# Layer 0 of a conv-attention hybrid: the second norm as a factor per token behind its linear layer, the projection's bias added by VectorE, and a new fixed order

## The chip, the cores and the metric

The kernel runs on one core of a Trainium2 chip. The metric is the device time of one execution in microseconds; the median of the runs is given. All tensors are float32.

## The reference, cut to what matters

The input x is 2 x 128 x 64 x 64 (images, channels, rows, columns). Layer 0 is a neighbourhood attention with a small feed-forward part, layer 1 is a full self-attention over the 4096 tokens of an image and a long filter. The change touches layer 0 alone:

```python
def _ln(x, g, b):
    mu = jnp.mean(x, -1, keepdims=True)
    var = jnp.mean((x - mu) ** 2, -1, keepdims=True)
    return (x - mu) * jax.lax.rsqrt(var + 1e-05) * g + b

r = x
y = _ln(x, g1, be1)
y = _na2d(y, qkv_w, qkv_b, rpb, proj_w, proj_b)   # 7x7 window, 4 heads; ends with out @ proj_w.T + proj_b
y = _ln(y, g2, be2)
y = y @ w1.T + bl1
x = y + r
r = x
y = _ln(x, g3, be3)
y = y @ w2.T + bl2
y = jax.nn.relu(y)
y = _ln(y, g4, be4)
y = y @ w3.T + bl3
x = y + r
```

The input of this is a group norm of x, and its result is added to x. Each norm is over the 128 channels of one token.

## The kernel before, in words

**Bands.** Layer 0 works on 16 bands: 2 images times 8 groups of 8 rows, 512 tokens each. Channels lie on the partitions (128 x 512); a norm over channels therefore transposes the band into four tiles of 128 tokens x 128 channels, takes mean and variance per token, and transposes back. Gains of the norms are multiplied into the weights once at the start, and the norms' constant terms become biases (`weights`, line 702 on).

**Pieces.** The work of a band is cut into named pieces. `p.*` makes the first norm and q, k, v (v goes to DRAM, `vd`, and comes back as windows, `vw`, through SP's queue). `u0` to `u3` are four units of 128 queries: `S` scores, `t0`-`t3` bias tables and row minimum on VectorE (line 517), `e0`-`e3` exp on ScalarE (line 527), `T0`, `T1` transposes (line 540), `c0`, `c1` their copies to SBUF (line 547), `V` the product with v (line 562). `r.*` scales by the denominators: `r.rb` on GpSimd (line 579), `r.rdT`, `r.c`, `r.att` (line 593). `t.*` is the rest:

- `t.proj` (lines 598 and 600): a 128 x 512 matmul of a one-hot row with `prow` puts the projection's bias into PSUM, four 128-column matmuls add onto it.
- norm `t1` (statistics `bn`, GpSimd's power `pw`, `nb`, `z` of two token tiles on ScalarE `za`, of two on VectorE `zd`, four transposes `tr`, copy `zT`), linear `t.w1`, residual `t.x2` (line 614).
- `t.tx` transposes x2 to tokens, norm `t2`, linear `t.w2` (line 331), `t.y` Relu with bias on ScalarE (line 635), `t.ty` transposes y to tokens (line 326), norm `t3`, `t.w3`, `t.fin` adds onto x.
- `t.add` on GpSimd (lines 624 and 626) adds the last bias and the outer residual to x2 in place.

`k.*` (bands 8 to 15 only) prepares layer 1's tokens of image 0: `k.a`, `k.tt`, `k.bn`, `k.pw`, `k.z` (GpSimd, line 683), `k.b` (transposes), `k.cm`.

**Order.** TensorE, VectorE, ScalarE and GpSimd each run a fixed order. The table `PLAN` gives each piece a time within a band's course; band k's pieces are shifted by k times `PERIOD`, all pieces are sorted by that time, and each engine executes its instructions in this order. So pieces of up to six bands are mixed. The first two bands' `p` pieces, the weights (`w`), the flips of the position table (`f0`-`f3`) and the table subtractions (`tab`) follow the list `FIRST`. Pieces of the last bands beyond a certain point (63 of them) are left to the attention of layer 1, whose loop calls three of them at each step; there the order is the compiler framework's. PSUM has five banks for most pieces, two more for some transposes and the projection, and one for `V`.

**Start.** SP issues eight DMAs for x of image 0 (line 126), then weights, the table rows (line 276), the masks and later x of image 1; ScalarE's queue issues the table rows of head 0 (line 278). The group norm's statistics come from x as it lands.

Of the kernel before, what the change touches and what calls it, by code (L numbers as in the profile page):

```python
# [14 lines left out]
P = 128  # L15
NB = 2
T = 4096
# [31 lines left out]

PLAN = {  # L50
    "p.xg": -4624, "p.tok": -4623, "p.bn": -4585, "p.pw": -4482, "p.zd": -4151, "p.nb": -3839, "p.za": -3660,
    "p.tr": -3511, "p.zT": -3413, "p.q": -3201, "p.k": -2932, "p.kT": -2885, "p.qT": -2796, "p.v": -2549,
    "p.vc": -2382, "u0.S": 0, "u0.t1": 36, "u0.t3": 47, "u0.t0": 54, "u0.t2": 62, "u0.e1": 108, "u0.e3": 138,
    "u0.e2": 138, "u0.e0": 219, "u0.T1": 464, "k.a": 508, "u0.T0": 531, "k.tt": 547, "u0.c0": 647, "u0.c1": 737,
    "u1.S": 780, "u1.t2": 906, "u1.t0": 946, "u1.t1": 951, "u1.t3": 1087, "u1.e1": 1088, "k.bn": 1103,
    "u2.S": 1108, "u2.t3": 1115, "u1.e3": 1128, "u2.t1": 1198, "u2.t0": 1198, "u2.e3": 1200, "u2.t2": 1274,
    "u2.e1": 1310, "u2.e0": 1339, "u1.e2": 1405, "u2.e2": 1786, "u2.T0": 1850, "u2.T1": 1865, "u1.e0": 1890,
    "u2.c1": 1906, "u1.T0": 1940, "u1.T1": 1979, "u0.V": 1986, "u2.c0": 1990, "u1.c0": 2005, "u1.c1": 2060,
    "u3.S": 2115, "u1.V": 2198, "u3.t3": 2222, "u3.t2": 2233, "u3.t1": 2278, "u3.t0": 2278, "k.pw": 2308,
    "u3.e1": 2339, "u3.e0": 2364, "u3.e3": 2372, "u3.e2": 2384, "u2.V": 2397, "r.rden": 2420, "u3.T0": 2436,  # L60
    "r.rb": 2566, "u3.c0": 2608, "u3.T1": 2689, "u3.c1": 2783, "r.rdT": 2827, "r.c": 2898, "u3.V": 2937,
    "k.z": 3009, "r.att": 3184, "t.proj": 3500, "k.b": 3601, "t1.bn": 3713, "k.cm": 4033, "t1.pw": 4306,
    "t1.nb": 4348, "t1.zd": 4410, "t1.za": 4597, "t1.tr": 5531, "t1.zT": 5674, "t.w1": 6276, "t.x2": 6324,
    "t.tx": 6935, "t2.bn": 7341, "t2.pw": 7594, "t2.nb": 7773, "t.add": 7929, "t2.za": 7975, "t2.zd": 7996,
    "t2.tr": 8384, "t2.zT": 8719, "t.w2": 9610, "t.y": 9723, "t.ty": 10247, "t3.bn": 10697, "t3.pw": 10918,
    "t3.zd": 11092, "t3.nb": 11166, "t3.za": 11410, "t3.tr": 11496, "t3.zT": 11553, "t.w3": 11573,
    "t.fin": 11589,
# [5 lines left out]
    "gn p.xg0 p.xg1 p.tok0 f0 p.tok1 p.bn0 f1 p.bn1 p.pw0 w f2 p.zd0 p.nb0 p.za0 p.pw1 p.tr0 f3 p.zd1 p.nb1 p.za1 p.zT0"  # L73
    " tab p.tr1 p.v0 p.q0 p.k0 p.vc0 p.zT1 p.qT0 tab0 p.kT0 tab1 p.v1 p.k1 p.q1 p.vc1 p.kT1 p.qT1 tab2 tab3"
# [18 lines left out]
def kernel(  # L93
# [31 lines left out]
    for c in range(8):  # L125
        nc.sync.dma_start(out=xa[0][:, c * 512 : (c + 1) * 512], in_=xin[0, :, c * 512 : (c + 1) * 512])
# [12 lines left out]

    nc.gpsimd.memset(rev[:, 0].rearrange("p n m -> p (n m)"), 0.0)  # L140
    nc.vector.memset(rev[:, HEADS - 1, NTAB], 0.0)
# [3 lines left out]
    flip = const.tile([P, P], F32, name="flip")  # L145
    nc.gpsimd.memset(flip, 0.0)
    nc.gpsimd.affine_select(
        out=flip, in_=flip, compare_op=ALU.not_equal, fill=1.0, base=1 - P, pattern=[[1, P]], channel_multiplier=1,
# [72 lines left out]
    with l0a:  # L221
# [26 lines left out]
        def flipped(h):  # L248
            pb = l0_bank()
            for half in range(2):  # L250
                nc.tensor.matmul(
                    pb[half * 64 : (half + 1) * 64, 0 : NTAB * NTAB], lhsT=flip[0:64, 64:128],
                    rhs=rev[:, h, 0:NTAB].rearrange("p n m -> p (n m)"), start=True, stop=True,
                )
            nc.scalar.copy(base[:, h].rearrange("p n m -> p (n m)"), pb[:, 0 : NTAB * NTAB])
# [14 lines left out]
        for r in range(QT):  # L270
            lo = 6 - min(r, 6)
            src = bass.AP(
                rpb_pad.tensor, (RPR + r - 6) * RPW + 50, [[1, QT], [RPW, (HEADS - 1) * RPR - r // 7], [1, NTAB]]
            )
            rows_ = rev[r * QT : (r + 1) * QT].rearrange("p h n m -> p (h n) m")
            nc.sync.dma_start(out=rows_[:, RPR : HEADS * RPR - r // 7], in_=src)
            src = bass.AP(rpb_pad.tensor, (lo + r - 6) * RPW + 50, [[1, QT], [RPW, RPR - lo], [1, NTAB]])
            nc.scalar.dma_start(out=rows_[:, lo:RPR], in_=src)
        nc.sync.dma_start(out=mask, in_=nc.inline_tensor(_window_masks(), "window_masks").ap())
# [13 lines left out]
        e0 = wp.tile([P, P], F32, name="e0")  # L293
        nc.gpsimd.memset(e0, 0.0)
        nc.gpsimd.memset(e0[0:1, :], 1.0)
        prow = wp.tile([P, 4, P], F32, name="prow")
        nc.gpsimd.memset(prow.rearrange("p j c -> p (j c)"), 0.0)
        wg = w_sb
        cb = wp.tile([P, 6], F32, name="cb")
        C_Q, C_K, C_V, C_1, C_2, C_3 = range(6)  # L300
# [68 lines left out]
        def norm_pieces(stage, src):  # L369
# [11 lines left out]
            @piece(stage + "pw")  # L381
            def _(t, b, g):
                rs = t[stage + "rs"] = ls.tile([P, 4], F32, tag="ln_rs", name="ln_rs")
                nc.gpsimd.tensor_scalar(rs, t[stage + "mv"][:, :, 1], 1e-5, None, ALU.add)
                nc.gpsimd.tensor_tensor(rs, rs, mhalf[:, 0:4], ALU.pow)

# [38 lines left out]
        @piece("p.xg")  # L425
        def _(t, b, g):
            gm, grs = norms[b]
            eng = nc.vector if b == 0 and g < 2 else nc.gpsimd
            t["xg"] = bp.tile([P, BAND], F32, tag="xg", name="xg", bufs=5)
            for nat, til in ordered(xa[b][:, rows_of(g)], t["xg"]):  # L430
                eng.tensor_scalar(til, nat, gm, grs, ALU.subtract, ALU.mult)
# [62 lines left out]
        def unit_pieces(u):  # L494
# [40 lines left out]
            def half_pieces(ch):  # L535
# [9 lines left out]
                def _(t, b, g):  # L545
                    pT = t[f"{name}c{ch}"] = sp.tile([HK, 512], F32, tag=f"pT{ch}", name="pT")
                    (nc.vector.tensor_copy if ch else nc.scalar.copy)(pT, t[f"{name}T{ch}"][0:HK])
# [48 lines left out]
        def _(t, b, g):  # L596
            pt = t["pp"] = l0_bank(1)
            nc.tensor.matmul(pt, lhsT=e0, rhs=prow.rearrange("p j c -> p (j c)"), start=True, stop=False)
            for j in range(4):
                nc.tensor.matmul(  # L600
                    pt[:, j * P : (j + 1) * P], lhsT=t["att"][:, j * P : (j + 1) * P],
                    rhs=wg[:, W_PROJ : W_PROJ + P], start=False, stop=(j == 3),
                )

        norm_pieces("t1.", "pp")
# [14 lines left out]
        norm_pieces("t2.", "px")  # L620
# [8 lines left out]
        def _(t, b, g):  # L629
            t["p2"] = linear(W_2, t["t2.zT"])  # L630

        @piece("t.y")
        def _(t, b, g):
            t["y"] = bp.tile([P, BAND], F32, tag="y", name="y", bufs=1)
            nc.scalar.activation(t["y"], t["p2"], AF.Relu, bias=cb[:, C_2 : C_2 + 1])  # L635

        @piece("t.ty")
        def _(t, b, g):
            t["py"] = to_tokens(t["y"])

        norm_pieces("t3.", "py")
# [55 lines left out]
        def weights():  # L697

            for i, (lo, be, col, row) in enumerate((
                (W_QKV, V_BE1, V_QB, None), (W_QKV + P, V_BE1, V_KB, None), (W_QKV + 2 * P, V_BE1, None, R_VB),
                (W_1, V_BE2, None, R_BL1), (W_2, V_BE3, None, R_BL2), (W_3, V_BE4, V_BL3, None),
            )):
                pb = l0_bank()
                nc.tensor.matmul(
                    pb[:, 0:1], lhsT=w_sb[:, lo : lo + P], rhs=v_sb[:, be : be + 1], start=True, stop=row is None
                )
                if row is None:  # L710
                    nc.vector.tensor_tensor(cb[:, i : i + 1], pb[:, 0:1], v_sb[:, col : col + 1], ALU.add)
                else:
                    nc.tensor.matmul(pb[:, 0:1], lhsT=r_sb[:, row, :], rhs=ones[:, 0:1], start=False, stop=True)
                    nc.vector.tensor_copy(cb[:, i : i + 1], pb[:, 0:1])
            pb = l0_bank()
            nc.tensor.matmul(
                pb[0:1, 0:P], lhsT=cb[:, C_V : C_V + 1], rhs=w_sb[:, W_PROJ : W_PROJ + P], start=True, stop=True
            )
            for j in range(4):
                nc.vector.tensor_tensor(prow[0:1, j, :], pb[0:1, 0:P], r_sb[:, R_PROJ, :], ALU.add)  # L720
            for lo, hi, g in ((W_QKV, W_PROJ, V_G1), (W_1, W_2, V_G2), (W_2, W_3, V_G3), (W_3, 896, V_G4)):
                nc.vector.tensor_scalar(wg[:, lo:hi], w_sb[:, lo:hi], v_sb[:, g : g + 1], None, ALU.mult)

            nc.vector.tensor_scalar(cb[:, 0:1], cb[:, 0:1], -QSCALE, None, ALU.mult)

# [9 lines left out]
        for name, f in (  # L735
            ("gn", lambda: [None for _ in group_norm(0)]), ("w", weights),
# [5 lines left out]
        for i in range(8):  # L742
            events.append((2 * PERIOD + 600 * i, None, "", lambda ci=2 + i // 4, h=i % 4: table(ci, h, nc.gpsimd)))

# [8 lines left out]
        free = ("r.att", "t.x2", "t.y", "t.fin")  # L753
        held = (("r.att", "t.proj", 1), ("t.x2", "t.fin", 4), ("t.y", "t.ty", 1))
# [644 lines left out]
```

## Time and profile before

| what | us |
|---|---|
| median of the runs (2297.27 to 2300.91) | 2300.69 |
| the profiled execution | 2295.84 |
| its span | 2293.9 |
| first score matmul of layer 0 | 44.9 |
| first matmul of layer 1's attention | 386.8 |
| last linear of layer 0 (inside the attention) | 460.0 |
| first matmul of the filter stage | 1380.9 |

The page's first two parts, engines over the whole span and over 40 equal slices of 57 us:

```profile
PE 2213.5 (96%) x11976; PEld 1360.3 (59%) x11976; DVE 950.4 (41%) x3047; ACT 793.3 (35%) x1943; POOL 256.0 (11%) x342
## 2 busy tenths in 40 slices
PE   5999998999999999999999989999999999999998
PEld 3666665544454443545444436767767767777777
DVE  4788886432443346533333342222222232322233
ACT  2688885322322223222222222222222232322221
POOL 3455765100000000000000000000000000000000
PEclk8999999999999999999999999999999999999999
```

Each digit is a busy share in tenths. The first seven slices are layer 0: the only stretch in which VectorE, ScalarE and GpSimd are busy to more than half. PE is TensorE, DVE VectorE, ACT ScalarE, POOL GpSimd. A float32 matmul appears as two records, a transpose as one.

### The profile page before, as it was taken

How to read it: one execution, taken by the hardware profiler on the slowest of the kernel's cores; microseconds unless marked ns; L12 is line 12 of the kernel's file. 1: busy time of each engine (PE TensorE's matmuls, PEld its weight loads, DVE VectorE, ACT ScalarE, POOL GpSimd, SP SyncE). 2: the span in 40 equal slices, each digit the busy share in tenths (PEclk: the TensorE clock that was granted, in tenths of full speed). 3: DMA queues.
4: the chain of work that ended last, by engine and by line, in shares of the span. 5: the costliest groups of instructions: out<-in, count | busy, mean ns of one | idle time of the engine just before them, and what ended most of it. 6: DMA issues, size and time to landing. Idle time of an engine off the chain costs nothing.

```text
span 2293.9 us, 31982 instructions
## 1 busy us (share of the span) xinstructions
PE 2213.5 (96%) x11976; PEld 1360.3 (59%) x11976; DVE 950.4 (41%) x3047; ACT 793.3 (35%) x1943; POOL 256.0 (11%) x342
## 2 busy tenths in 40 slices
PE   5999998999999999999999989999999999999998
PEld 3666665544454443545444436767767767777777
DVE  4788886432443346533333342222222232322233
ACT  2688885322322223222222222222222232322221
POOL 3455765100000000000000000000000000000000
PEclk8999999999999999999999999999999999999999
DMA  4222123011100005200000024221221221212101
GB/s 118 62 55 55 53 54 58 5 42 65 37 1 24 23 23 144 70 24 0 24 23 23 23 69 104 57 52 44 57 57 39 56 50 45 57 38 58 38 10 74
DMA packets 181436, 109.79 MB, mean 48 GB/s; under 512 B 32289, under 2 KB 165921, under 8 KB 180770
## 3 DMA queue, kind: packets, MB, share of 16 engines
q1 hardware_dynamic: 180042, 107.65, 18.1%
q8 instruction: 95, 1.56, 0.3%
q14 instruction: 59, 0.48, 0.1%
q10 hardware_dynamic: 1240, 0.09, 0.0%
HBM read 73.09 MB, written 34.60 MB: 47 GB/s over the span
## 4 chain that ended last, share of the span: by engine, by line
PE 88%; DVE 5%; ACT 2%; POOL 1%; DMA 1%; issue 1%; SPq 0%; POOLq 0%; DVEq 0%; ACTq 0%
PE acc L1223 24%; PE pc L1212 12%; PE own L865 9%; PE bank L837 9%; PE other L890 8%; PE bank L851 4%; PE bank L331 3%; PE bank L540 2%; PE bank L190 2%; PE py L1250 2%; PE bank L982 2%; PE bank L950 2%; PE bank L1086 1%; PE po L562 1%; DVE p L517 1%; PE bank L504 1%
## 5 line engine op out<-in xcount | busy, mean ns | idle before, releaser
L1213 DVE COPY y<-pc 128x512 f32<-128x512 f32 x320 | 221.5, 692 | 358.7 <-PE pc L1212 355.0
L844 ACT ACTIVATE e<-bank 128x512 f32<-128x512 f32 x288 | 172.0, 597 | 567.1 <-PE bank L837 435.1
L837 PE MATMUL bank<-cm 128*128 128x512 f32 x576 | 296.9, 599 | 0.8 <-ACT y L635 0.8
L1212 PE MATMUL pc<-ct,ut 64*128 64x512 f32 x1280 | 287.7, 600 | 5.6 <-DMA ct<-gs 5.6
L1223 PE MATMUL acc<-y,mpl 128*128 128x256 f32 x1280 | 292.1, 382 | 0.0
L1223 PE MATMUL acc<-y,mmi 128*128 128x256 f32 x1280 | 288.0, 379 | 0.0
L1223 PEld LDWEIGHTS acc<-y,mpl 128*128 128x128 f32 x1280 | 238.3, 190 | 59.2 <-issue 29.5
L1223 PEld LDWEIGHTS acc<-y,mmi 128*128 128x128 f32 x1280 | 242.7, 190 | 32.5
L1213 ACT COPY y<-pc 128x512 f32<-128x512 f32 x320 | 204.9, 640 | 93.8 <-PE pc L1212 93.8
L865 PE MATMUL own<-et,tok 128*128 128x512 f32 x448 | 227.5, 594 | 2.3 <-DVE part L854 2.3
L890 PE MATMUL other<-e,tok 128*128 128x512 f32 x448 | 228.6, 592 | 0.0
L854 DVE CUSTOM_DVE_ANT_0 et<-bank,one 128x512 f32<-128x512 f32 x224 | 145.7, 688 | 165.3 <-PE bank L851 165.3
L1212 PEld LDWEIGHTS pc<-ct,ut 64*128 64x128 f32 x1280 | 122.1, 188 | 152.4 <-issue 147.2
L1229 ACT COPY ob<-acc 128x256 f32<-128x256 f32 x40 | 24.1, 602 | 431.2 <-PE acc L1223 431.2
L865 PEld LDWEIGHTS own<-et,tok 128*128 128x128 f32 x448 | 84.2, 190 | 111.1 <-issue 69.7
L890 PEld LDWEIGHTS other<-e,tok 128*128 128x128 f32 x448 | 85.2, 190 | 107.1 <-issue 107.1
L837 PEld LDWEIGHTS bank<-cm 128*128 128x128 f32 x576 | 96.0, 192 | 73.9 <-issue 43.7
L1262 DVE TENSOR_TENSOR xa<-py,xa 128x512 f32<-128x512 f32 x32 | 22.1, 692 | 281.4 <-PE py L1250 281.4
L851 PEld LDWEIGHTS bank<-ident,e 128*128 128x128 f32 x896 | 103.2, 141 | 53.0 <-issue 44.6
L162 POOL TENSOR_TENSOR ln_rs<-ln_rs,mhalf 128x4 f32<-128x4 f32 x24 | 24.3, 1011 | 878.3 <-DVE ln_rs L161 878.3
L527 ACT ACTIVATE p<-p,mn 128x196 f32<-128x196 f32 x256 | 114.6, 452 | 22.1 <-DVE mn L517 22.1
L851 PE MATMUL bank<-ident,e 128*128 128x128 f32 x896 | 116.9, 273 | 0.0
(187 smaller groups left out, 2374.5 us busy)
## 6 DMA issues: line engine op xcount, KB each, us to landing
ut<-us SPq DMA_DIRECT2D x80, 256.0 KB
us<-ub SPq DMA_DIRECT2D x64, 256.0 KB
vw<-vd SPq DMA_DIRECT2D x256, 49.0 KB
ct<-gs SPq DMA_DIRECT2D x160, 72.0 KB
ct<-gs SPq DMA_DIRECT2D x160, 64.0 KB
gs<-ub SPq DMA_DIRECT2D x20, 256.0 KB
vd<-v SPq DMA_DIRECT2D x128, 32.0 KB
st<-in_m_plus_dram SPq DMA_DIRECT2D x16, 256.0 KB
```

What stands on the lines that cost most here:

```text
L190: nc.tensor.transpose(ps[:, j * P : (j + 1) * P], src[:, j, :], ident)
L331: nc.tensor.matmul(pl, lhsT=wg[:, lo : lo + P], rhs=zT, start=True, stop=True)
L527: nc.scalar.activation(p, p, AF.Exp, bias=t[name + "mn"][:, h : h + 1], scale=-1.0, accum_out=t["den"][:, u, h : h + 1],)
L837: nc.tensor.matmul(ps, lhsT=cm[b][:, n * P : (n + 1) * P], rhs=cm[b][:, chunk(c)], start=True, stop=True)
L844: nc.scalar.activation(e, ps, AF.Exp, bias=0.0, scale=ASCALE, accum_out=part[:, n, c : c + 1])
L851: nc.tensor.transpose(pt[:, k * P : (k + 1) * P], es[k][:, m * P : (m + 1) * P], ident)
L854: nc.vector.tensor_tensor_reduce(et, pt, one, 1.0, 0.0, ALU.mult, ALU.add, part[:, n, a : a + 1])
L865: nc.tensor.matmul(own, lhsT=tok[b][:, n, :], rhs=e, start=first, stop=last)
L890: nc.tensor.matmul(other, lhsT=tok[b][:, 4 * CHUNKS[a] + j, :], rhs=es[j], start=(j == 0), stop=(j == 3))
L1212: nc.tensor.matmul(pc, lhsT=ut[fp, b, par, :], rhs=cv_[fp], start=True, stop=True)
L1213: (nc.scalar.copy if f else nc.vector.tensor_copy)(y[:, 4 * f : 4 * f + 4, :, par, b * 2 * FB + q : (b + 1) * 2 * FB : 2], pc.rearrange("p ...
L1223: nc.tensor.matmul(acc, lhsT=(mmi if l else mpl)[:, k, :], rhs=y[:, 1::2, k, ::-1, :] if l else y[:, 0::2, k, :, :], start=(l == 0 and k = ...
```

## The change

1. **Projection.** The one-hot bias matmul is gone. A new piece `t.pb` on VectorE adds a bias tile (the same row on all partitions, repeated for four token tiles) to the projection's PSUM and writes `x1` to SBUF. Norm `t1` reads `x1`.
2. **Second norm.** Only its statistics and power stay (`t2.bn`, `t2.pw`). `t.w2` multiplies x2 itself, as four 128-column matmuls with the tokens as output rows, by weights from which the mean over the input channels is taken out (the mean's subtraction is in the weights). `t.y` on VectorE multiplies each token's row by its factor and adds a bias row (four 128 x 128 instructions); a new piece `t.yr` on GpSimd takes the maximum with 0. The result is in token layout, so `t.ty` is gone, and `t2.nb`, `za`, `zd`, `tr`, `zT` are gone. Norm `t3` reads `y` from SBUF.
3. **Copies.** `c1` of units 1 and 3 moves from VectorE to ScalarE.
4. **Start.** x comes by four DMAs of 512 KB. The table rows' memsets (now both on GpSimd) and DMAs are issued after the averaging matrix is made. The flip matrix gives both halves by one 128-row matmul instead of two of 64 rows. xg of band 2 is made by VectorE. Of the weights' products only those of q, k, v come first; the rest (`behind`) follow in four portions after the first units.
5. **Order.** `PLAN` and `FIRST` are new in all places; 65 pieces are left to the attention.

```diff
-    for c in range(8):
-        nc.sync.dma_start(out=xa[0][:, c * 512 : (c + 1) * 512], in_=xin[0, :, c * 512 : (c + 1) * 512])
+    for c in range(4):
+        nc.sync.dma_start(out=xa[0][:, c * 1024 : (c + 1) * 1024], in_=xin[0, :, c * 1024 : (c + 1) * 1024])
...
-    "gn p.xg0 p.xg1 p.tok0 f0 p.tok1 p.bn0 f1 p.bn1 p.pw0 w f2 p.zd0 p.nb0 p.za0 p.pw1 p.tr0 f3 p.zd1 p.nb1 p.za1 p.zT0"
-    " tab p.tr1 p.v0 p.q0 p.k0 p.vc0 p.zT1 p.qT0 tab0 p.kT0 tab1 p.v1 p.k1 p.q1 p.vc1 p.kT1 p.qT1 tab2 tab3"
+    "gn p.xg0 p.xg1 p.tok0 p.tok1 w f0 p.bn0 p.bn1 f1 p.pw0 p.pw1 p.zd0 p.nb0 p.za0 p.tr0 f2 p.zd1 p.nb1 p.za1 p.tr1 f3"
+    " wd p.zT0 tab p.v0 p.q0 p.k0 p.zT1 p.vc0 p.qT0 tab0 p.kT0 p.v1 p.k1 p.q1 p.vc1 p.kT1 p.qT1 tab1 tab2 tab3"
...
-            eng = nc.vector if b == 0 and g < 2 else nc.gpsimd
+            eng = nc.vector if b == 0 and g < 3 else nc.gpsimd
...
-                    (nc.vector.tensor_copy if ch else nc.scalar.copy)(pT, t[f"{name}T{ch}"][0:HK])
+                    (nc.vector.tensor_copy if ch and u % 2 == 0 else nc.scalar.copy)(pT, t[f"{name}T{ch}"][0:HK])
...
-            nc.tensor.matmul(pt, lhsT=e0, rhs=prow.rearrange("p j c -> p (j c)"), start=True, stop=False)
             for j in range(4):
                 nc.tensor.matmul(
                     pt[:, j * P : (j + 1) * P], lhsT=t["att"][:, j * P : (j + 1) * P],
-                    rhs=wg[:, W_PROJ : W_PROJ + P], start=False, stop=(j == 3),
+                    rhs=wg[:, W_PROJ : W_PROJ + P], start=True, stop=True,
                 )
...
+        @piece("t.pb")
+        def _(t, b, g):
+            t["x1"] = bp.tile([P, 512], F32, tag="x1", name="x1", bufs=2)
+            nc.vector.tensor_tensor(
+                t["x1"].rearrange("p (j c) -> p j c", c=P), t["pp"].rearrange("p (j c) -> p j c", c=P), added(0), ALU.add
+            )
...
-        norm_pieces("t1.", "pp")
+        norm_pieces("t1.", "x1")
...
-        norm_pieces("t2.", "px")
+        statistics_pieces("t2.", "px")
...
-            t["p2"] = linear(W_2, t["t2.zT"])
+            t["p2"] = l0_bank()
+            for j in range(4):
+                nc.tensor.matmul(
+                    t["p2"][:, j * P : (j + 1) * P], lhsT=t["x2"][:, j * P : (j + 1) * P], rhs=wg[:, W_2:W_3],
+                    start=True, stop=True,
+                )
...
-            t["y"] = bp.tile([P, BAND], F32, tag="y", name="y", bufs=1)
-            nc.scalar.activation(t["y"], t["p2"], AF.Relu, bias=cb[:, C_2 : C_2 + 1])
-
-        @piece("t.ty")
-        def _(t, b, g):
-            t["py"] = to_tokens(t["y"])
-
-        norm_pieces("t3.", "py")
+            t["y"] = bp.tile([P, 512], F32, tag="y", name="y", bufs=2)
+            for j in range(4):
+                js = slice(j * P, (j + 1) * P)
+                nc.vector.scalar_tensor_tensor(
+                    t["y"][:, js], t["p2"][:, js], t["t2.rs"][:, j : j + 1], add[:, 1, :], ALU.mult, ALU.add
+                )
+
+        @piece("t.yr")
+        def _(t, b, g):
+            nc.gpsimd.tensor_scalar(t["y"], t["y"], 0.0, None, ALU.max)
+
+        norm_pieces("t3.", "y")
...
+        def behind():
+
+            pb = l0_bank()
+            products_(pb, C_1, W_1, V_BE2, R_BL1)
+            products_(pb, C_3, W_3, V_BE4, None)
+            for i, col in enumerate((cb[:, C_V : C_V + 1], v_sb[:, V_BE3 : V_BE3 + 1])):
+                nc.vector.tensor_copy(wide[:, i, :], col.to_broadcast([P, P]))
+            yield
...
+            nc.vector.tensor_copy(add.rearrange("p i c -> p (i c)"), pb[:, 0 : 2 * P])
+            for lo, hi, g in ((W_1, W_2, V_G2), (W_2, W_3, V_G3), (W_3, 896, V_G4)):
+                gains(lo, hi, g)
+            yield
+            pb = l0_bank()
+            nc.tensor.matmul(pb[:, 0:P], lhsT=centre, rhs=wg[:, W_2:W_3], start=True, stop=True)
+            nc.vector.tensor_copy(wg[:, W_2:W_3], pb[:, 0:P])
+            yield
```

From the new `PLAN`, the pieces from a band's `u1.T1` to its `u3.S`, in TensorE's order with the band offset, where bands 8 to 15 are at work: `u1.T1`, `p.k+2`, `u0.V`, `p.q+2`, `k.b-1`, `u2.T1`, `u2.T0`, `p.v+2`, `u3.S`.

## The prediction

> **What bounds the kernel now.** I read the busy table by stage first, then the order of TensorE within one band, then the waits, then rows for single instructions. By stage (columns: stretch in us, its length, then busy us and instruction count of TensorE, its weight loads, VectorE, ScalarE, GpSimd, and the granted clock, DMA share, GB/s):
>
> ```profile
> 0.00:44.90 44.90, 24.73 (x90) 14.34 (x90) 20.10 (x71) 8.28 (x15) 18.41 (x38) 0.99 0.49 134
> 44.90:386.80 341.90, 316.75 (x4504) 220.91 (x4503) 282.54 (x1393) 261.47 (x820) 199.05 (x261) 0.97 0.20 55
> 470.00:1400.00 930.00, 903.42 (x2962) 435.96 (x2961) 364.06 (x1105) 255.95 (x640) 24.25 (x24) 0.99 0.15 42
> 1400.00:2293.90 893.90, 886.96 (x4149) 646.71 (x4147) 249.19 (x352) 239.85 (x392) 0.00 (x0) 1.00 0.20 49
> ```
>
> The change touches layer 0 alone: the start, the bands (first score matmul at 44.9 to first attention matmul at 386.8), and the last pieces of layer 0 that run inside the attention up to about 460. From there on nothing is different. In the bands TensorE is busy 93%, VectorE 83%, ScalarE 76%, GpSimd 58%. The broadcasts of the denominators (one per band, line 579) start 20.2 us apart in bands 4 to 7 and 21.0 to 21.3 later, where each band also prepares four token tiles of layer 1. So a band costs what TensorE needs, but VectorE is not far behind: 43.6 of every 50 us from 150 to 250, or 17.6 us per band.
>
> TensorE in order of time, one band (start us, busy us; the gap to the next start is what a group really costs, because ends are modelled):
>
> ```profile
> 210.25 0.62 PE L326 MATMUL bank<-ident,y 128*128 128x128 f32 x4
> 210.70 0.60 PE L190 MATMUL bank<-ident,z 128*128 128x128 f32 x4
> 211.23 0.63 PE L504 MATMUL bank<-kT,qT 32*64 32x196 f32 x16
> 212.65 1.10 PE L598 MATMUL bank<-prow,e 128*128 128x512 f32 x2 [0.79 <-ACT p L527]
> 213.58 1.05 PE L600 MATMUL bank<-w_sb,att 128*128 128x128 f32 x8
> 214.47 1.02 PE L331 MATMUL bank<-zT,w_sb 128*128 128x512 f32 x2
> 215.34 0.60 PE L190 MATMUL bank<-ident,z 128*128 128x128 f32 x4
> ```
>
> Four transposes cost 0.44 us (210.25 to 210.70; 215.34 to 215.77), the bias matmul of the projection 0.93 (212.65 to 213.58), one 512-column linear 0.87, the same work as four 128-column matmuls 0.89 (line 600). The only large repeated wait is the 0.79 ahead of the bias matmul.
>
> **TensorE, per band.** Removed: the bias matmul 0.93; the transposes of y back to tokens 0.45; the transposes of the second norm's z 0.44; the 512-column second linear 0.87. Added: four 128-column matmuls 0.89. Net 0.93 + 0.45 + 0.44 + 0.87 - 0.89 = **1.80 us per band, 28.8 us over 16 bands**. About 3.1 of it lies in pieces that the kernel before runs inside the attention (one bias matmul, three y transposes, two z transposes there); TensorE is the bound there too, so it counts in full.
>
> **VectorE, per band.** Rows (mean ns of one):
>
> ```profile
> L547 DVE COPY pT<-bank 98x512 f32<-98x512 f32 x64 | 42.9, 685 | 7.7 <-PE po L562 3.9 <-PE bank L540 3.0
> L410 DVE TENSOR_SCALAR z<-bank,ln_mv,ln_rs 128x128 f32<-128x128 f32 x112 | 40.3, 402 | 10.5 <-ACT z L401 7.9 <-POOL ln_rs L385 2.5
> L593 DVE TENSOR_TENSOR att<-po,rdT 128x512 f32<-128x512 f32 x16 | 11.1, 692 | 10.9 <-ACT pT L547 9.4 <-PE po L562 1.5
> ```
>
> and, from the start, the same operation as z but with its source in SBUF:
>
> ```profile
> L722 DVE TENSOR_SCALAR w_sb<-w_sb,v_sb 128x128 f32<-128x128 f32 x3 | 0.7, 268 | 0.0
> ```
>
> Added: the projection's bias, one 128x512 add from PSUM, 0.69 by line 593. The scaled bias of the second linear is four 128x128 scalar_tensor_tensor ops; no such row, so from both sides: 0.75 if four cost as one (line 614, 128x512, 747 ns), 1.16 if each costs as the 128x128 add of line 650 (291 ns); I take 1.0. Removed: two z halves of the second norm, 0.64 from the pair's start to the next instruction (211.78 to 212.42); its nb 0.12; two of four pT copies, which go to ScalarE for odd units, 2 x 0.60. Also z of norms 1 and 3 now reads SBUF: 4 x (402 - 268) = 0.54 less. Sum 1.69 - 0.64 - 0.12 - 1.20 - 0.54 = -0.8.
>
> **ScalarE, per band.** Gone: Relu 0.69, two z quarters 0.81, one zT copy 0.58; added two pT copies 2 x 0.58. About -0.9. Not the bound.
>
> **GpSimd, per band.** The new ReLU is a 128x512 tensor_scalar in SBUF. Rows:
>
> ```profile
> L683 POOL TENSOR_SCALAR tok<-tt,kmv,krs 128x128 f32<-128x128 f32 x32 | 25.1, 793 | 0.1
> L624 POOL TENSOR_SCALAR x<-x,cb 128x512 f32<-128x512 f32 x15 | 23.6, 1575 | 1.3 <-PE bank L326 1.3
> L579 POOL COPY rb<-rden 128x512 f32<-128x512 f32 x16 | 9.8, 610 | 17.8 <-DVE rden L574 17.8
> ```
>
> Line 624 is the same operation and shape: 1.57. The Trainium skill ("GPSIMD Engine Reference", section 4.1, Engine selection) sends elementwise max to VectorE and calls one-input work on GpSimd roughly line rate; with its 1.2 GHz that is an estimate of 0.43 for 512 columns. The row disagrees by 3.6 times and decides. Where it matters: in bands 8 to 15 the order on GpSimd is rb, power of the second norm, ReLU, residual adds, k.z, and TensorE then stands at k.b, the transposes of k.z's result. After rb GpSimd needs 1.27 + 1.57 + 3.0 + 3.13 = 9.0 us; TensorE's own work from rdT to k.b (4+8 transposes for rdT and unit 0, V, two S, t1 transposes, projection, w1, p transposes, eight unit-1 transposes, k, V, q) sums to 9.3. By the row the cover is 0.3 us, by the rule it would be 1.4. With semaphores and late releases I put **0.5 us of new wait per band there, 4 us in eight bands** (by the rule: 0).
>
> A second rule speaks against the change: "SBUF — State Buffer", section "Who interferes with whom", says VectorE in its two-port mode, or with two SBUF inputs against a GpSimd read, and GpSimd lock each other out for a whole instruction. The trace has a case: the tab subtractions take 342 ns on VectorE alone and up to 655 while GpSimd does the same (and 558 to 707 on GpSimd). z of norms 1 and 3 was free of it (PSUM source) and now isn't. GpSimd's instructions from one rb to the next (247.35 to 268.61) sum to 15.5 us; with the ReLU it is busy about 17 of 19.4, with instructions whose mean remainder, weighted by length, is about 0.5: by the rule an estimate of 0.8 us per band on VectorE; by the row of line 722 alone, 0. I take 0.8, which eats VectorE's gain: it stays near 17.6 in a band of 18.4, covered but with under 1 us to spare.
>
> **The start.** Before, units of band 0 wait for this chain:
>
> ```profile
> 33.37 7.98 POOL L260 TENSOR_TENSOR tab<-tok 128x196 f32<-128x196 f32 x13 [4.02 <-ACT tok L255]
> 44.20 0.73 PE L326 MATMUL bank<-ident,xg 128*128 128x128 f32 x3 [1.68 <-POOL xg L431]
> 44.86 0.33 PEld L504 LDWEIGHTS bank<-kT,qT 32*64 32x64 f32 x16 [0.33 <-issue]
> ```
>
> Band 2's xg sits behind 13 table ops on GpSimd; now VectorE makes it (0.69), after band 1's kT. The weight block's products (21.6 to 26.6) and the two-half flips (4 x 1.6) ahead of the first z transposes shrink to four matmuls and 4 x 0.8. x comes by four DMAs of 512 KB (the later four issued in 2.04 us, the eight before in 7.11), so SP reaches the weights and table rows some 3 us sooner, ahead of the 16 vd writes that still follow v. ScalarE's eight table DMAs, issued from 1.26 on, now wait for GpSimd's two memsets behind the averaging matrix, which end some 2 us later; the first flip stands after the weight products, at 18 or so, and hides that. Walked through with these rows, the first score matmul is at 38 to 39. Against that, the postponed products (about 12 small matmuls, 4 us at the rows' cold 0.58 per pair) fall between band 0's units, where TensorE is idle a third of the time: 1.5 lost. **Start: -5** (0 to -8).
>
> **The end of the bands.**
>
> ```profile
> 380.74 0.90 PE L190 MATMUL bank<-ident,z 128*128 128x128 f32 x4 [2.10 <-ACT z L401]
> 382.31 3.68 PE L331 MATMUL bank<-zT,w_sb 128*128 128x512 f32 x4 [0.67 <-ACT zT L423]
> 386.77 4.56 PE L837 MATMUL bank<-cm 128*128 128x512 f32 x10 [0.78 <-ACT y L635]
> ```
>
> From the last V (373.2) to the attention are 13.6 us with 4.8 of TensorE work in them: 8.8 of waiting for norm chains. The new order keeps only t1 transposes, w1, k.b and w2 there (2.6 us of work); I estimate 4 of waiting (k.z 1.5, zT 0.7, y before banks come free 1.1, more). **-5.**
>
> **Sum**: -28.8 - 5 - 5 + 4 = -34.8. The profiled execution took 2295.84 (span 2293.9), so 2261 against its own time. The median shown, 2300.69, lies 4.85 above; as a median, **2266**. Its own range, from the bounds above (start 0 to -8, k.b wait 0 to 8, end -2 to -7): 2257 to 2278.
>
> **Rivals.**
> *VectorE becomes the bound.* It now idles 2.6 us per band in waits that are loops with ScalarE and TensorE (line 593 waiting for ScalarE's pT copy 9.4, z 7.9, p 6.6). If these 2.6 stay, its 17.6 makes 20.2 again and the bands gain nothing; left are 3.1 + 5 + 5 = 13: 2288. For it: the thin margin. Against: these waits are mostly there because VectorE runs ahead of TensorE. 0.15.
> *GpSimd makes it slower.* Place: TensorE at k.b behind k.z. The 9.0 us must grow past 9.3 plus what the change saves elsewhere, (34.8 + 4)/8 = 4.9 per band, so from about 14 us on the total is a loss; with every GpSimd op stretched 1.7 times by the port lock it would be 15.3, or 8 x (15.3 - 9.3) = 48 against 38.8: 2310. Before, no line-624 op was stretched beyond 1597 ns. 0.04.
> *More than the sum.* The 0.79 wait ahead of the bias matmul goes with it, since the projection now stands elsewhere in TensorE's order: 16 x 0.7 more, and no k.b wait: 2251. 0.11.
>
> Forecast 0.70. The range holding 8 of 10: 2251 to 2288. A measurement of this kernel tells about 0.2% (4.6 us; the three runs spread 3.6). Faster 0.94, same 0.02, slower 0.04.
>
> **What would show it.** Band spacing of line 583 (the old 579) near 18.5, then 19.4; no wait of note at k.b; ReLU at 1.57 and z from SBUF at 0.27 (or stretched towards 1: the lock); first score matmul at 38 to 39; 6 to 7 us from last V to the attention. Spacing still above 20 with VectorE over 90% would make me wrong by the first rival.

## The result and the profile after

| | before | after |
|---|---|---|
| median of four runs each, us | 2298.98 (2294.67 to 2300.91) | 2275.87 (2274.97 to 2279.68) |
| ratio, with 95% interval | | 0.9905 (0.9886 to 0.9925) |
| the profiled execution's span | 2293.9 | 2274.0 |

The kernel became 23 us faster, about 1%. The forecast was 2266 (2251 to 2288), 34.8 less than the 2300.69 of its base: right side, inside the range, but a third of the gain is missing. The profiled executions, 19.9 us apart, tell where. "rb" is the broadcast of the denominators, once per band (line 583 after):

| stretch, us | before | after | measured | forecast |
|---|---|---|---|---|
| start of the span to the first rb | 65.78 | 66.69 | +0.9 | -5 |
| first to last rb: the bands | 305.60 | 275.13 | **-30.5** | -21.7 |
| last rb to the first attention matmul: the handover | 15.39 | 16.84 | +1.5 | -5 |
| attention, to the first filter matmul | 994.16 | 1002.08 | **+7.9** | -3.1 |
| filter, to the end | 912.97 | 913.26 | +0.3 | 0 |

(The -28.8 on TensorE is split here: 3.1 lies in pieces left to the attention, so the bands' forecast is -28.8 + 3.1 + 4 for the wait at `k.b`.) The bands gave more than was forecast; start, handover and attention gave 23.4 less than forecast.

The page's first two parts, after:

```profile
PE 2194.0 (96%) x11908; PEld 1355.6 (60%) x11908; DVE 936.9 (41%) x3047; ACT 784.2 (34%) x1911; POOL 275.9 (12%) x354
...
PE   6999998999999999999999979999999999999998
...
DVE  4799984333443336533333433222223232232323
ACT  2889883222332233222222223223223232232222
POOL 3377874200000000000000000000000000000000
PEclk8999998999999999999999989999999999999999
```

TensorE has 19.5 us less to do. In the layer's slices VectorE and ScalarE are now busier and GpSimd reaches 8. The clock row has an 8 in the seventh slice, that of the handover, where before had a 9. (A second one, the 24th slice, 1308 to 1364, is the end of the attention with the step into the filter stage.) Busy time by stretch, 50 us of bands 4 to 7 and then of bands 8 to 11 (columns as in the stage table of the prediction):

```profile
150.00:200.00 50.00, 50.00 (x796) 37.39 (x795) 47.55 (x247) 45.22 (x141) 35.56 (x43) 1.00 0.22 59
200.00:250.00 50.00, 49.84 (x769) 37.41 (x767) 47.63 (x258) 45.47 (x141) 41.91 (x54) 1.00 0.23 63
```

In before the first of these stretches had TensorE at 47.6 and VectorE at 43.6. Now TensorE has no gap and VectorE is at 95%. The rows of the new operations and of those that the forecast re-priced, with shapes kept apart:

```profile
L661 POOL TENSOR_SCALAR y<-y 128x512 f32<-128x512 f32 x16 | 24.0, 1499 | 0.0
L655 DVE SCALAR_TENSOR_TENSOR y<-bank,ln_rs,add 128x128 f32<-128x128 f32 x64 | 17.8, 338 | 2.4 <-PE bank L645 2.4
L414 DVE TENSOR_SCALAR z<-y,ln_mv,ln_rs 128x128 f32<-128x128 f32 x32 | 11.8, 406 | 0.0
L414 DVE TENSOR_SCALAR z<-bank,ln_mv,ln_rs 128x128 f32<-128x128 f32 x32 | 11.4, 397 | 1.0 <-POOL ln_rs L385 1.0
L414 DVE TENSOR_SCALAR z<-x,ln_mv,ln_rs 128x128 f32<-128x128 f32 x32 | 11.2, 391 | 0.0
L614 DVE TENSOR_TENSOR x<-bank,add 128x512 f32<-128x512 f32 x16 | 11.1, 691 | 1.9
```

The ReLU takes 1.50 (1.57 taken), the bias add 0.69 (0.69). z from SBUF is in the mean no faster than z from PSUM. By these rows only z was much dearer than thought, and VectorE's share of a band still fell (17.1 us, 47.55 of 50 in a band of 18.01); the missing time sits in the order.

**The handover.** TensorE in order of time:

```profile
346.44 0.65 PE L566 MATMUL po<-pT,vw 98*32 98x64 f32 x32
...
352.83 1.91 PE L645 MATMUL bank<-w_sb,x 128*128 128x128 f32 x8
358.66 6.16 PE L892 MATMUL bank<-cm 128*128 128x512 f32 x10 [3.92 <-DVE seen L1075]
...
412.74 1.70 PE L920 MATMUL own<-et,tok 128*128 128x512 f32 x2 [2.11 <-DVE part L909]
```

The first line is the last product with v. Then, after some norm and `k.b` transposes, `t.w2` of one band, and a wait of 3.92 us that ended with VectorE. VectorE itself:

```profile
347.84 0.15 DVE L1061 TENSOR_TENSOR z<-lw,gu 128x4 f32<-128x4 f32 x1
354.98 0.30 DVE L377 BATCH_NORM_STATS2 ln_st<-y 128x6 f32<-128x128 f32 x1 [6.99 <-POOL y L661]
...
357.39 1.12 DVE L655 SCALAR_TENSOR_TENSOR y<-bank,ln_rs,add 128x128 f32<-128x128 f32 x4
358.43 0.14 DVE L1075 COPY seen<-oh 128x1 f32<-128x1 f32 x1
```

VectorE stands for 7 us at the statistics of one band's y, released by the ReLU. Behind it in VectorE's fixed order stand another band's residual and `t.y` (line 655), which empty PSUM banks, and the attention's own small operations. And GpSimd:

```profile
346.18 1.57 POOL L637 TENSOR_SCALAR x<-x,cb 128x512 f32<-128x512 f32 x1 [3.76 <-PE bank L645]
...
349.36 3.15 POOL L705 TENSOR_SCALAR tok<-tt,kmv,krs 128x128 f32<-128x128 f32 x4
352.47 1.01 POOL L639 TENSOR_TENSOR x<-x,xa 128x384 f32<-128x384 f32 x1
353.44 1.51 POOL L661 TENSOR_SCALAR y<-y 128x512 f32<-128x512 f32 x1
```

The ReLU's input was ready when line 655 of 346.11 (four instructions, not shown) had ended, at 347.2. It ran at 353.4, behind the last tokens of `k.z` and the residual adds. That is the chain: GpSimd's queue holds the ReLU, the ReLU holds VectorE, VectorE holds TensorE. The granted clock is low too, in the ten us that hold the wait and in the twenty that hold the one of 2.11:

```profile
350.00:360.00 10.00, 4.65 (x14) 3.18 (x15) 3.56 (x20) 0.77 (x3) 8.18 (x11) 0.59 0.00 0
400.00:420.00 20.00, 17.89 (x65) 9.59 (x64) 9.21 (x38) 3.67 (x11) 6.87 (x8) 0.91 0.00 0
```

Before, the ten us of its handover (380 to 390) kept 0.83.

**The start.** TensorE, with the DMA issues of SP below:

```profile
17.42 1.70 PE L248 MATMUL bank<-cm,flip 64*128 64x400 f32 x2
22.50 1.67 PE L248 MATMUL bank<-cm,flip 64*128 64x400 f32 x2 [3.38 <-DMA cm<-in_rpb_pad_dram]
...
32.89 2.08 PE L465 MATMUL bank<-w_sb,zT 128*128 128x128 f32 x8 [1.07 <-ACT zT L427]
...
44.17 0.70 PE L508 MATMUL bank<-kT,qT 32*64 32x196 f32 x16
```

```profile
6.11 10.97 SPq L289 DMA_DIRECT2D cm<-in_rpb_pad_dram  x8
```

Before, the same eight issues ran from 10.10 to 16.66 (6.56 us). They now begin 4 us sooner and end at 17.1, so the second flip waits for its rows until 22.5 and the first transposes of z, next in TensorE's order, wait with it. ScalarE stands at the copy of this flip for 4.56 us, with its part of z behind it. What SP itself waited for (us in total, times, longest):

```profile
SPq L289 <- DMA v_sb<-in_vecs_dram: 4.6, 1, 4.6
```

`v_sb` is a small transfer of weights, issued at 3.43 behind x and the weight block; the second of the eight issues waits on its semaphore until 11.04. Before, the second issue ran at 11.09. The first scores start at 44.2 instead of 44.9; 38 to 39 was forecast.

### The profile page after: what moved, and what is told of

Read it like the earlier page. It is cut to its first block, busy times and chain, and to the rows that moved or that the text cites. A ratio compares the mean times of both kernels' runs of the same rounds, so it can differ in the third digit from the quotient of the medians.

```text
span 2274.0 us, 31748 instructions
## 1 busy us (share of the span) xinstructions
PE 2194.0 (96%) x11908; PEld 1355.6 (60%) x11908; DVE 936.9 (41%) x3047; ACT 784.2 (34%) x1911; POOL 275.9 (12%) x354
## 3 DMA queue, kind: packets, MB, share of 16 engines
q8 instruction: 94, 1.54, 0.3%
## 4 chain that ended last, share of the span: by engine, by line
PE 86%; DVE 6%; POOL 4%; DMA 1%; ACT 1%; issue 1%; SPq 0%; POOLq 0%; DVEq 0%; ACTq 0%
PE acc L1278 25%; PE pc L1267 13%; PE own L920 10%; PE bank L892 9%; PE other L945 8%; PE bank L906 4%; PE bank L331 2%; PE py L1305 2%; PE bank L188 2%; PE bank L1037 2%; PE bank L544 2%; PE bank L1005 2%; PE bank L1141 1%; PE bank L508 1%; DVE ln_st L377 1%
```

## The experiments

The theory after the result was: the bands do what the sum says; the ReLU on GpSimd is harmless inside the bands and costs some 10 us where they hand over; the flips ahead of band 0's q, k, v cost the start. The rivals: VectorE is the bound and holds the bands; the operations, not the order, are what the gain is made of; the handover is slow whoever does the ReLU. All times below are medians; the ratio is to the kernel before, in runs on the same chip. The kernel after was not run again beside e1 to e8; the medians of before lie within 1.1 us of each other (2298.70 to 2299.77). Stretches (us) are those of the table above, from one profiled execution each:

| kernel | median | ratio (95%) | first rb | bands | handover | attention |
|---|---|---|---|---|---|---|
| before | 2298.98 | | 65.78 | 305.60 | 15.39 | 994.16 |
| after | 2275.87 | 0.9905 (0.9886 to 0.9925) | 66.69 | 275.13 | 16.84 | 1002.08 |
| e1, late ReLU | 2267.66 | 0.9861 (0.9846 to 0.9875) | 66.06 | 276.54 | 12.80 | 994.31 |
| e2, every ReLU | 2265.05 | 0.9859 (0.9842 to 0.9875) | 66.05 | 271.60 | 14.58 | 997.05 |
| e3, flips later | 2271.48 | 0.9875 (0.9860 to 0.9890) | 59.80 | 278.34 | 15.15 | 998.52 |
| e4, extra matmul | 2283.45 | 0.9930 (0.9915 to 0.9945) | 67.60 | 284.26 | 15.15 | 1001.57 |
| e5, e2 and e3 | 2258.92 | 0.9829 (0.9815 to 0.9844) | 60.45 | 272.99 | 14.59 | 997.31 |
| e6, old order | 2287.43 | 0.9951 (0.9937 to 0.9964) | 69.29 | 296.91 | 13.74 | 993.53 |
| e7, ReLU twice | 2289.40 | 0.9958 (0.9943 to 0.9973) | 69.56 | 288.82 | 17.11 | 999.06 |
| e8, e5 and k.z | 2258.55 | 0.9823 (0.9810 to 0.9837) | 60.88 | 275.14 | 13.73 | 992.77 |

The first rb of kernels with the same `FIRST` differs by up to 3.5 us (66.05 in e2 to 69.56 in e7), and their first scores lie between 43.8 and 47.1, so a start is read to some 3 us only. The spacing of rb within bands 4 to 7 is steadier: 18.0 in every kernel with the new order but e3 (18.2) and e4.

**e1: the ReLU of the last four bands on VectorE.**

```diff
-            nc.gpsimd.tensor_scalar(t["y"], t["y"], 0.0, None, ALU.max)
+            (nc.vector if b and g > 3 else nc.gpsimd).tensor_scalar(t["y"], t["y"], 0.0, None, ALU.max)
```

> The changed kernel with the ReLU of bands 12 to 15 (all of them pieces left to the attention) on VectorE; everything else stays. Theory (the handover lost its gain because VectorE's statistics of y stood in order behind a ReLU that waited in GpSimd's queue): from the last V to the first attention matmul 6 to 8 us instead of 12.2, the 7.0 us wait of VectorE on the ReLU gone, the clock of the first attention slices back near 1.0; 2266 to 2270 against 2275.9, ratio to before 0.986 to 0.988. Rival (the handover is held by the banks and by the branch weights' DMAs): first attention matmul at the same distance, 2274 to 2278.

8.2 us less than after, and the attention at 994.3 (before 994.2); the bands gain nothing (+1.4, all of it in one spacing). TensorE's first attention matmuls:

```profile
355.40 7.36 PE L892 MATMUL bank<-cm 128*128 128x512 f32 x10 [1.38 <-DVE zm L1070]
363.20 1.13 PE L920 MATMUL own<-e,tok 128*128 128x512 f32 x2 [0.44 <-ACT e L899]
```

The 3.92 us wait has become 1.38, and in 400 to 420 TensorE has no wait and a clock of 1.00 instead of 0.91. The wait of 3.9 us ahead of the first attention matmul and the one of 2.1 some 54 us later stand in every kernel with the new order and the late ReLU on GpSimd (after, e3, e4, e7) and in none of the others. So they do come from the ReLU's place in GpSimd's queue.

Two parts of the expectation failed. From the last product with v (345.55) to the attention are still 9.9 us, not 6 to 8: what remains there is not the ReLU's. And the clock in 350 to 360 is 0.54, no better than after. Nor is all of the attention's loss the ReLU's. By ScalarE's exps, counted from the first attention matmul, the kernel after is 5.4 us behind the kernel before up to the change of images (at some 880 us), 7.4 behind that, and 7.9 at the filter. The 5.4 is 5.3 in e4 and e7 and 3.7 in e3, but 0.0 to 0.2 in e1, e2 and e5: this part goes with the ReLU. The other 2.5 is 2.7 in e2 and 2.9 in e5, but 0.1 in e1 and -0.4 in e7: it does not. e1's profiled execution, the fastest of its four, lacks it; its median is 3.1 higher.

**e2: every ReLU on VectorE.** The same line with `nc.vector` alone.

> The changed kernel with the ReLU of all bands on VectorE. If GpSimd's cover at k.b is what limits bands 8 to 15, they get shorter (19.05 to about 18.7 us) and the total is 3 us below the version with only the late ones moved; if VectorE is near its bound in the bands, its 0.4 us per band (128x512 from SBUF) lengthens the bands of 18.0 us by up to that, 3 to 5 us above that version; if neither is near, the same within 1 us.

VectorE's instruction takes 0.42 us in the median against GpSimd's 1.50. VectorE in bands 8 to 11, second stretch of the busy table:

```profile
200.00:250.00 50.00, 50.00 (x774) 37.70 (x773) 49.28 (x268) 46.05 (x142) 39.90 (x53) 1.00 0.23 62
```

It is at 98.6% and the bands became faster, not slower: rb to rb over bands 9 to 12 is 18.53 against 19.04 after, and 18.02 against 18.01 in bands 4 to 7, where no `k.z` stands in GpSimd's queue. With 0.42 us more work per band VectorE lengthens no band, so it did not bound the kernel after, and the ReLU's price in bands 9 to 12 is 0.5 us per band. In the whole run it is less: bands, handover and attention together are 1283.2, in e1 1283.6. In this profile 1.8 of the bands' gain is gone in the handover and 2.7 between the change of images and the filter (in 1310 to 1320 the clock is 0.83, in e1 1.00). The medians of e2 and e1 are 2.6 apart, and the ranges of their runs overlap.

**e3: flips and table behind q, k, v of band 0** (the first list; the rest of the kernel as after).

```diff
-    "gn p.xg0 p.xg1 p.tok0 p.tok1 w f0 p.bn0 p.bn1 f1 p.pw0 p.pw1 p.zd0 p.nb0 p.za0 p.tr0 f2 p.zd1 p.nb1 p.za1 p.tr1 f3"
-    " wd p.zT0 tab p.v0 p.q0 p.k0 p.zT1 p.vc0 p.qT0 tab0 p.kT0 p.v1 p.k1 p.q1 p.vc1 p.kT1 p.qT1 tab1 tab2 tab3"
+    "gn p.xg0 p.xg1 p.tok0 p.tok1 w p.bn0 p.bn1 p.pw0 p.pw1 p.zd0 p.nb0 p.za0 p.tr0 p.zd1 p.nb1 p.za1 p.tr1"
+    " wd p.zT0 p.v0 p.q0 p.k0 p.zT1 p.vc0 p.qT0 p.kT0 f0 f1 p.v1 p.k1 p.q1 p.vc1 f2 f3 tab tab0 p.kT1 p.qT1 tab1 tab2 tab3"
```

> The changed kernel with another order of the first steps: the four flips and the table subtractions stand behind q, k, v of band 0 instead of ahead of the first transposes. Theory (the start gained nothing because TensorE and ScalarE wait at the second flip, to 22.5 us, for the table rows' DMAs, whose issue ends at 17.1 as before): first v matmul at 22 to 25 instead of 32.9, first score matmul at 37 to 40 instead of 44.2, total 4 to 6 us shorter: 2270 to 2272. Rival (the granted clock of 0.50 from 45 to 55 us and the windows' DMAs set the start): first scores earlier, but the first denominators stay at 66 to 67, total the same within 1 us.

```profile
22.75 2.00 PE L465 MATMUL bank<-w_sb,zT 128*128 128x128 f32 x8
...
26.39 1.61 PE L248 MATMUL bank<-cm,flip 64*128 64x400 f32 x4
...
36.71 0.96 PE L508 MATMUL bank<-kT,qT 32*64 32x196 f32 x16
```

v of band 0 starts 10.1 us sooner (22.75), the first scores 7.5 (36.71) and the first rb 6.9. The forecast start was there to be had, with another list. The bands give 3.2 of it back, 2.5 of that in the last spacing (21.2); the profiled execution is the fastest of this kernel's four, and by medians 4.4 remain.

**e4: one more 128 x 512 matmul per band**, ahead of the projection, whose result the projection overwrites.

```diff
             pt = t["pp"] = l0_bank(1)
+            nc.tensor.matmul(pt, lhsT=ident, rhs=t["att"], start=True, stop=True)
```

> The changed kernel with one more 128x512 matmul per band ahead of the projection (its result is overwritten), the size of the bias matmul that the change removes. If TensorE alone bounds the bands: 0.86 to 0.93 us per band, bands 18.9 and 19.95 us apart, total 14 to 15 us longer, 2290. If VectorE or the loops between engines bound them: 0 to 5 us.

Bands 4 to 7: 18.88 per band, +0.87, the matmul's full 0.86. Bands 9 to 12: 19.38, +0.34. In the first TensorE sets the pace alone. In the second it sets only part of it. In all 7.6 us, half of the 14 to 15 that TensorE as the only bound would have cost.

**e5: e2 and e3 together.**

> The flips behind q, k, v of band 0 and the ReLU of all bands on VectorE, together. The two act in different stages (start; bands 8 to 15 and handover), so if both causes are right they add: 2275.9 - 7 - 10.5 = 2258, ratio to before 0.982. If the start's gain is lost again later (as the last bands and the clock took part of it in the version with the flips alone), 2263 to 2266.

2258.92: e2 and e3 gained 10.8 and 4.4 over after, together 17.0. The two parts do not stand in each other's way.

**e6: the new operations in the old order** (the old `PLAN` without the removed pieces, with the two new ones put in; everything else as after).

The lines against the table of before, cut:

```diff
+    "t.pb": 3650,
...
+    "t.yr": 9780,
...
-    "t2.nb": 7773, "t2.za": 7975, "t2.zd": 7996, "t2.tr": 8384, "t2.zT": 8719, "t.ty": 10247,
```

> The new operations in the old table of times (the removed pieces struck out, the projection's bias 150 behind the projection, the ReLU 57 behind y; the start as in the changed kernel). If the operations alone make the bands shorter: 20.2 - 1.8 = 18.4 us in bands 4 to 7 and 19.3 in bands 8 to 15, total as the changed kernel within 4 us. If the new order carries the gain: bands above 19.3 and 20.3, total above 2285.

```profile
150.00:200.00 50.00, 47.55 (x706) 34.25 (x704) 44.04 (x223) 40.85 (x129) 33.68 (x40) 1.00 0.22 59
```

19.30 per band in bands 4 to 7 (before 20.21, after 18.01) and 20.84 in 9 to 12 (21.19, 19.04). TensorE has less to do, but stands idle 2.45 of 50 us as it did before; it waits for band tiles of x and for `k.z` from GpSimd. So of the 2.2 us per band that the change gains in bands 4 to 7 the operations alone give 0.9, and the order the other 1.3. (No run has the old operations in the new order, so another division is possible.) With this order the ReLU, on GpSimd too, does no harm at the handover (13.74, attention 993.53, both below before): the loss there takes the ReLU on GpSimd and the new order together.

**e7: the ReLU of bands 0 to 11 done twice on GpSimd** (the second leaves y unchanged).

```diff
             nc.gpsimd.tensor_scalar(t["y"], t["y"], 0.0, None, ALU.max)
+            if not (b and g > 3):
+                nc.gpsimd.tensor_scalar(t["y"], t["y"], 0.0, None, ALU.max)
```

> The changed kernel with the ReLU of bands 0 to 11 done twice on GpSimd (1.5 us more per band on GpSimd, the late bands unchanged). If GpSimd's queue ends last at k.b in bands 8 to 15, as the version with the ReLU on VectorE (18.5 instead of 19.05 us) suggests: nothing in bands 4 to 7 (18.0), and about 1.5 us more in each band in which k.b follows (20.5), some 10 to 12 us in all, 2286 to 2288. If GpSimd had cover left: under 4 us.

Bands 4 to 7: 18.02, unchanged. Bands 9 to 12: 20.58, +1.54, the full price of a ReLU. There a longer GpSimd queue costs its full length, with no slack, while e2 showed that 1.5 less gives only 0.5: the kernel after stands close to where GpSimd and TensorE are equally long. The waits between 130 and 330, total, count and longest, after:

```profile
DVE ln_nb L394 <- POOL ln_rs L385: 8.1, 10, 1.7
...
PE bank L188 <- POOL tok L705: 0.9, 2, 0.5
```

and with the ReLU twice:

```profile
DVE ln_nb L394 <- POOL ln_rs L385: 17.3, 10, 3.3
...
PE bank L188 <- POOL tok L707: 4.7, 9, 1.2
```

GpSimd's lateness shows mainly at VectorE (+9.2), which stands at a norm's shift for GpSimd's power, and less at TensorE at `k.b` (+3.8).

**e8: e5, and k.z of the last band on VectorE**, to take the 3.15 us of `k.z` out of the handover (the edit beside that of e5).

```diff
-                nc.gpsimd.tensor_scalar(
+                (nc.vector if g == NG - 1 else nc.gpsimd).tensor_scalar(
                     tok[0][:, t["n0"] + j, :],
```

> The version with flips and ReLU moved, and in addition k.z of band 15 alone (four 128x128 instructions, 0.78 us each on GpSimd) on VectorE. In the handover TensorE waits 1.02 + 0.47 + 0.30 + 0.30 us between k.b's four transposes for GpSimd. If k.z is what remains of the handover: last V to first attention matmul 7.0 to 7.5 instead of 9.5 us, 2256 to 2257. If the first attention matmul waits for VectorE's branch weights in any case: 9 to 9.5, 2258 to 2259.

2258.55 against 2258.92: no gain. From the last product with v to the attention are 10.8 us, more than either outcome that was expected (10.0 in e5). TensorE still waits at the handover, as its timeline shows, and GpSimd's beneath it:

```profile
349.75 6.23 PE L892 MATMUL bank<-cm 128*128 128x512 f32 x10 [3.19 <-DVE y L655]
```

```profile
343.57 2.91 POOL L1058 TENSOR_TENSOR sg<-sg,quarter 128x16 f32<-128x16 f32 x1
```

Now a power of layer 1's setup (2.91 us) stands in GpSimd's queue ahead of the norm's power, VectorE stands 2.61 us for that power at the norm's shift (line 394), and `t.y` stands behind it. It is the same chain with another link.

e5 and e8, at 2258.9 and 2258.6, beat both kernels; between them there is nothing to choose.

## Why the prediction was right, and where it was wrong

The sum came out in the range partly by luck. The bands gave 8.8 us more than their terms, mostly by the gaps that the new order closed, and start, handover and attention gave 23.4 less; without the first, about 11 us of the 34.8 would have been left.

**TensorE, -1.80 per band: the direction holds, the gain is only in part its own.** Bands 4 to 7 gained 2.2 per band. That TensorE sets the pace there is shown by e4 (full price). But the term took TensorE's saved work as the whole gain. By e6, in the old order it brings 0.9 per band, half of the term; the other 1.3 comes from an order that leaves TensorE no gaps. The idle 2.4 in 50 us of the kernel before was in the busy table, and the forecast did count one case for it (the 0.79 wait goes, "more than the sum", 0.11). In the bands it was that case; in the total it was not.

**The wait at k.b, +0.5 per band: mechanism right, place a little off.** TensorE stood at `k.b` for 0.9 us in 200. But GpSimd's queue did bound the bands with `k` pieces, by 0.5 per band (e2), and with no slack (e7), through VectorE's norm shift more than through `k.b` itself. The duration of the ReLU was right because the row decided: 1.50, three and a half times the 0.43 estimated from the Trainium skill ("GPSIMD Engine Reference", section 4.1). The other half of the same rule, that an elementwise maximum belongs on VectorE, was the one that spoke against this change, and e1 and e2 bear it out: moving it gains 8 to 11 us.

**VectorE, net -0.8 and then +0.8.** Of the terms, z from SBUF is the one that failed: 268 ns was taken from a row whose operation has one scalar per partition, where z has two; the measured means are 391 and 406, beside 397 from PSUM. The trace of after separates two parts. Between 60 and 330 us, 17 of these 50 ran with no GpSimd instruction beside them, all in 332 to 343 ns; the 18 beside GpSimd's `xg` (line 435) have a mean of 415, and four beside rb took 632 to 634 (others beside GpSimd were not slowed). So some 70 ns over the row belong to z alone; GpSimd's company adds 62 in the mean, an estimate of 0.25 us for the four of a band, where 0.8 stood for all of VectorE. The four `t.y` take 1.12 (1.0). The forecast left VectorE near 17.6 us per band, and it needs 17.1. For bands 8 to 15 it read too low: its 43.6 of 50 holds from 150 to 200, from 200 to 250 it was 45.35, or 19.2 of a band of 21.2; after it is 18.1 of 19.04. It does not bound the bands: e2 adds work to it and no band grows. The first rival falls.

**The start, -5: wrong, +0.9.** Two terms of the walk failed. The merged flip was to cost 0.8 instead of 1.6 per head; it costs 1.70 (line 248 at 17.42), as much as the two half flips together (1.59, before). In the trace of before the two halves start 0.006 us apart (16.830 and 16.836): they ran side by side, so there was nothing to halve. And "SP reaches the weights and table rows some 3 us sooner" held for the weights (2.65 instead of 7.95) and the first row only: the second row's DMA waited 4.6 us for `v_sb`, so the last was no sooner. The walk took issue times from a trace without that wait. e3 shows that the flips and the table ahead of q, k, v were what kept band 0 back: 6.9 us at the first rb.

**The end of the bands, -5: wrong, +1.5, and +7.9 in the attention where -3.1 was forecast.** This is the step that cost most, and e1 shows the greater part of its cause. The step counted TensorE's work left in the handover and the norm chains' waits. It took 4.8 us of the 13.6 from the last product with v to the attention as work and 8.8 as waiting. But 4.8 is what this work costs at the steady gaps (five groups of transposes at 0.44, three linears at 0.87); in the trace of before TensorE was busy 8.7 there, at a granted clock of 0.87, and idle 4.9, so there was less waiting to win. Measured from there the stretch went to 12.2 (5.7 busy, 6.5 idle), not to 6 or 7. And the step did not walk GpSimd's queue past the last `k.z` as it did for the bands, although the ReLU had been priced and VectorE's statistics stand right behind it. There was no TensorE work left to cover it, and one late ReLU held the residual, the PSUM banks and the first scores of the next layer. Some 6.5 us went in the handover and 11 in the attention against the forecast; of these the ReLU's are 4.0 (e1's handover) and 5.4, and by the medians 8.2 in all. e1 does not reach the forecast either (handover -2.6, attention +0.15 against before); e8 shows what comes next, a power in GpSimd's queue. That a free handover exists with these operations was not shown.

At the change of images TensorE waits 2.92 us for a norm of layer 1 in after, 1.89 in before, and the clock fell to 0.66 for ten us; about 2.5 us of the attention's +7.9 arise from there on. This is not the handover's doing: the same wait is 2.92 in e6 and 2.83 in e2, where the ReLU costs nothing at the handover, and 1.87 in e1. Why it differs is open.

## What to carry to other kernels

When a step is moved to another engine, walk that engine's queue at each place where the step occurs, the last pieces above all: a price that is covered in the steady bands has no cover where TensorE runs out of work. In-order engines pass a delay on: ask what is queued behind the instruction that waits, and who waits for that. And where the operations change together with their order, price the gaps that the bound engine has as well as the work that it loses.

## What the runs showed of the hardware

- The granted clock was low where TensorE waited, but not by the length of one wait: 0.59 in the ten us that hold the 3.92 us wait (350 to 360) and 0.66 in those with 2.92 (876 to 886), yet 0.54 in e1's 350 to 360, where no wait is above 1.38, and 1.00 in the ten us around a wait of 3.42 in e4 (882 to 892). The Trainium skill ("TensorE: Matmul & The Clock Gate", Part 1) puts the limit at an idle window of some 3.4 us; as a limit on single waits that does not come out of these runs.
- One 128-row flip took 1.70 us per head at 17.42, and 0.80 (four records in 1.61) at 26.39 in e3. TensorE had worked without a gap for 3.65 us before the first and for 5.57 before the second, and both stretches show a granted clock of 1.00. Durations at a start are not the steady ones, whatever that column says.
- SP's eight issues of table rows took 6.56 us when they began at 10.10 and 10.97 when they began at 6.11. In the second case 4.6 us are one wait for `v_sb`, issued at 3.43 while x was on its way (412 GB/s from 4 to 8 us). A DMA that is issued sooner can stand in SP's queue for an earlier one to land: the second row was issued at 11.04 instead of 11.09.
- Two half flips (64 x 64) start 0.006 us apart and take 1.59 us together, one whole flip 1.70: two narrow matmuls side by side cost no more than the wide one.
